# A two-layer graph network on one core: node products made ahead of the neighbour lists, the last lists made inside layer 0

## The chip, the cores and the metric

The kernel runs on one NeuronCore of a Trainium2 chip. The core has a matrix engine (PE, whose weight loads are shown apart as PEld), a vector engine (DVE), a scalar engine (ACT), GpSimd (POOL) and a sync engine (SP) that here only issues transfers. Sixteen DMA engines move data between HBM and the on-chip memory SBUF. [...] The metric is the device time of one execution in microseconds, the median of several.

## The reference: what is computed

Inputs are 4096 nodes with 512 features (x), a 4096 x 4096 matrix adj of 0 and 1 in int32 (64 MB, about four ones in a row), and weights.

```python
# layer 0: attention with 8 heads of 64
Wh = einsum('nf,hfo->hno', x, W)
f1 = einsum('hno,ho->hn', Wh, a[:, :64]); f2 = einsum('hno,ho->hn', Wh, a[:, 64:])
e  = where(adj > 0, leaky_relu(f1[:, :, None] + f2[:, None, :], 0.2), -9e15)
x  = layernorm(x + softmax(e) @ Wh)
# layer 1: mean of the neighbours, two linear maps and a third over both
agg = (adj > 0) @ x / max(deg, 1)
out = concat([x @ W_self + b_self, agg @ W_nb + b_nb]) @ W_comb + b_comb
x   = layernorm(x + relu(out))
```

## The kernel before: tiling, stages and order

The kernel does not multiply by adj. It turns each row of adj into a short list of neighbours and then gathers rows. Nodes are worked in 32 blocks of 128. The instruction order on every engine is the order of the program text (`manual_schedule`), each engine works its own instructions in that order, and waits between engines follow from the data and from the reuse of buffers.

1. *Start.* w_sb holds W with 16 more columns, the products of W with the two halves of a, so that one matmul gives f2, Wh and f1 together. DVE makes these columns (L722, L727). PE multiplies W_nb by the lower half of W_comb into m2 (`fold_weights`, L251 and L262) and the bias (`fold_bias`, L279): layer 1 then needs one product with m2 and one with m1 instead of four.
2. *Lists* (loop at L746, one step a block). SP loads adj in halves of 1 MB (`load_adj`, four buffers, so two blocks) and x eight blocks ahead. ACT turns a half into 0 and 1 in bf16 (`mask_adj`, L367), waiting for its transfer. PE turns x (`transposed`, L304; ACT copies the result), makes the node row in two halves (`node_half`, L312) and between them packs the mask into keys (`fold_adj`, L379). DVE copies the halves into a row (L316) and finds the largest keys (`max_keys`, L393). The row goes to the table t0 in HBM by a transfer that ACT issues; rows have two buffers, so a row waits for the transfer of the one before the last. Every fourth step starts a `decode` of four blocks: a generator of DVE work, of which one part is done in each of the next steps (L402 to L487) with two small PE products (L436, L463). Its results are the indices to gather (idx), the extra places of rows with over three neighbours (es) and the degrees. A node with more than three neighbours borrows one of 256 extra places of its block.
3. *The turn.* When the last row of t0 is in HBM, POOL starts the gathers of t0 (`gather`, L508: five indirect transfers a block). DVE finishes the decodes of the last eight blocks, and PE makes m1 from W_self and the upper half of W_comb, one piece at a time.
4. *Layer 0* (loop at L800, step i works on blocks i-1 to i+3 at different stages). DVE forms attention weights (`a_weights`: L532 for the first three neighbours, L536 for the extra places) and weighs the gathered rows (L580 to L611); PE adds the extra places (L595) and sums of weights (L546); ACT does exp and the normalization (L618 to L627); PE turns the new x block and multiplies it by m2 (`a_z`, L632), and the result goes to the table t1 in HBM.
5. *Layer 1* (loop at L876). Gathers of t1, the product with m1 (`g_self`, L656), the extra places (L663), mean, relu and normalization.

A flag tells at the end whether the short form was allowed (at most 256 extra places, values in bounds); otherwise a dense form runs, which these inputs do not reach.

Of the kernel before, what the change touches and what calls it, by code (L numbers as in the profile page):

```python
# [39 lines left out]
P = 128  # L40
# [7 lines left out]
K0 = 3  # L48
# [36 lines left out]
def listed_layers(  # L85
# [32 lines left out]
    EX = KX + 2 + 1 + H  # L118
# [89 lines left out]
    es = const.tile([P, NB, KH, EX], F32, name="es")  # L208
    idx = const.tile([P, NB, KS], U32, name="idx")
# [4 lines left out]
    m1 = const.tile([P, FB, HD], F32, name="m1")  # L214
    brow = const.tile([P, HD], F32, name="brow")
    bc = const.tile([1, HD], F32, name="bc")
# [13 lines left out]
    def load_fold(k, w, fp):  # L230
        wr = fp.tile([P, FB, HD], F32, name="wr")
        (nc.sync, nc.scalar)[k].dma_start(wr, w.rearrange("(c p) o -> p c o", p=P))
        wc = fp.tile([P, FB, HD], F32, name="wc")
        (nc.sync, nc.scalar)[k].dma_start(
            wc, w_comb[k * HD : (k + 1) * HD, :].rearrange("(c p) o -> p c o", p=P)
        )
        return wr, wc
# [6 lines left out]
    def fold_weights(loaded, m, wp, tag="pw", last=None):  # L244

        wr, wc = loaded

        def turned(c):
            tp = ps.tile([P, FB, P], F32, name="nm", bufs=2)
            for d in range(FB):  # L250
                nc.tensor.transpose(tp[:, d, :], wr[:, c, ts(d, P)], ident)  # L251
            t = wp.tile([P, FB, P], F32, name="xT", bufs=2)
            nc.scalar.copy(t, tp)
            return t

        wT = turned(0)
        for c in range(FB):
            nxt = turned(c + 1) if c + 1 < FB else last and last()
            t = "pw" if c + 1 < FB else tag
            mp = ps.tile([P, HD], F32, name=t, bufs=2 if t == "pw" else 1)  # L260
            for d in range(FB):
                nc.tensor.matmul(  # L262
                    mp, lhsT=wT[:, d, :], rhs=wc[:, d, :], start=(d == 0), stop=(d == FB - 1)
                )
                if t != "pw" and d == FB // 2 - 1:
                    yield
            nc.scalar.copy(m[:, c, :], mp)
            wT = nxt
            yield

    def fold_bias(loaded, brw, to, tag):
# [5 lines left out]
        bp = ps.tile([1, HD], F32, name=tag, bufs=1)  # L277
        for d in range(FB):
# [4 lines left out]
            if d == FB // 2 - 1:  # L283
                yield
        nc.vector.tensor_add(brow[0:1, :], bp, to)
# [9 lines left out]
    def load_x(b, xacc):  # L295
        if b < NB:
            nc.sync.dma_start(xs[:, b, :], x[ts(b, P), :])
            nc.gpsimd.tensor_tensor(xacc, xacc, xs[:, b, :], OP.add)  # L298
# [19 lines left out]
    def node_rest(b, row):  # L318
# [3 lines left out]
        )  # L322

    def mean_row(w_sb, xacc, wp):
# [7 lines left out]
        nc.vector.tensor_copy(xm, pm)  # L332
        mr = wp.tile([P, HD], F32, name="y", bufs=2)
        mf = small.tile([1, H], F32, name="mf", bufs=1)
        for k in range(2):
# [9 lines left out]
            if k == 0:  # L345
                nc.vector.tensor_copy(mf, pq[:, 0:H])
        nc.scalar.dma_start(t0[1:2, 0:H], mf)
        nc.scalar.dma_start(t0[1:2, H:TW], mr[0:1, :])

# [3 lines left out]
    def load_adj(b, ap):  # L353

        if b < NB:
            for h in range(NH):
                at = loads[b, h] = ap.tile([P, NG // NH, SC], I32, name="at", bufs=4)
                r = b * P + h * (P // NH)
                nc.sync.dma_start(
                    at, adj[r : r + P // NH, :].rearrange("(j r) (s c) -> (r s) j c", r=RG, s=SEG)  # L360
                )

    def mask_adj(b, h, ap):
        if b == NB:
            return
# [29 lines left out]
    def decode(b0, dp, wp):  # L395
# [48 lines left out]
        if b0 + G == NB:  # L444
            yield
        for b in range(b0, b0 + G):
            lt = wp.tile([P, KH * P], F32, name="st", bufs=2)
            nc.vector.tensor_scalar(lt, iota[:, 0 : KH * P], end[:, b : b + 1], None, OP.is_lt)
            if b0 + G < NB:
                st = wp.tile([P, KH * P], F32, name="own", bufs=4)  # L450
            else:
                if b % 2 == 0:
                    rows = wp.tile([P, FW], F32, name="row", bufs=2)
                st = rows[:, b % 2 * KH * P : (b % 2 + 1) * KH * P]
# [5 lines left out]
        pe = ps.tile([P, G, KH, EX], F32, name="sm", bufs=2)  # L460
# [6 lines left out]
        if b0 + G == NB:  # L467
            yield
        nc.vector.tensor_copy(es[:, bs], pe)
# [35 lines left out]
    def gather(table, b, gp):  # L505
        g = gp.tile([P, KS, TW], F32, name="g")
# [22 lines left out]
    def a_weights(b, wp):  # L529
        gw = G0[b][:, :, 0:H]  # L530
        e = E[b] = wp.tile([P, KS, H], F32, name="e", bufs=3)
        nc.vector.tensor_tensor(  # L532
            e[:, 0:K0, :], gw[:, 0:K0, :],
            lst[:, b, KL + 3 :].unsqueeze(1).to_broadcast([P, K0, H]), OP.add,
        )
        nc.vector.tensor_add(e[:, K0:KS, :], gw[:, K0:KS, :], es[:, b, :, KX + 3 :])  # L536
# [149 lines left out]
    wp = ctx.enter_context(tc.tile_pool(name="work", bufs=1))  # L686
    dp = ctx.enter_context(tc.tile_pool(name="decode", bufs=1, side="right"))
    ap_cm = tc.tile_pool(name="lists", bufs=1, side="right")
    ap = ap_cm.__enter__()
    xa = ctx.enter_context(tc.tile_pool(name="xa", bufs=1))  # L690
    xacc = xa.tile([P, FIN], F32, name="xacc")
    nc.gpsimd.memset(xacc, 0.0)
    w_sb = xa.tile([P, FB, FW], F32, name="w_sb")
    with tc.tile_pool(name="wa", bufs=1) as wa:
        arow = wa.tile([1, H, 2, D], F32, name="arow")
        nc.scalar.dma_start(arow, a0.rearrange("h (k d) -> h k d", k=2).unsqueeze(0))
        for h in range(H):
            nc.sync.dma_start(
                w_sb[:, :, H + h * D : H + (h + 1) * D], w0[h].rearrange("(c p) o -> p c o", p=P)
            )  # L700
        loaded = load_fold(1, w_nb, wa)
        brw = load_bias(1)
        nc.scalar.dma_start(bc, b_comb.rearrange("(a o) -> a o", a=1))
        load_x(0, xacc)
        load_x(1, xacc)
        load_adj(0, ap)
        load_x(2, xacc)
        load_x(3, xacc)
        load_adj(1, ap)
        for b in range(4, XL):  # L710
            load_x(b, xacc)
        pads(wp)
        av = []
        for k in range(2):
            av.append(ps.tile([P, H, D], F32, name=("key", "sm")[k], bufs=(1, 2)[k]))
            nc.tensor.matmul(av[k], lhsT=oner, rhs=arow[:, :, 1 - k, :], start=True, stop=True)
        for a in range(2):
            for k in range(2):
                for c in range(FB):
                    pr = wa.tile([P, H // 2, D], F32, name="pr", bufs=2)  # L720
                    cs = slice(H + a * HH, H + (a + 1) * HH)
                    nc.vector.tensor_mul(  # L722
                        pr, w_sb[:, c, cs].rearrange("p (h d) -> p h d", d=D),
                        av[k][:, a * 4 : a * 4 + 4, :],
                    )
                    f = k * TW + a * 4
                    nc.vector.tensor_reduce(w_sb[:, c, f : f + 4], pr, AX.X, OP.add)  # L727
        last = {}

        def first():  # L730
            last["xT"] = transposed(0, wp)

        pieces = fold_weights(loaded, m2, wp, last=first)
        for c in range(FB):
            next(pieces)
            if 1 <= c <= 2:
                mask_adj(0, c - 1, ap)
        next(pieces, None)
        for _ in fold_bias(loaded, brw, bc, "key"):
            pass  # L740
    fp = ctx.enter_context(tc.tile_pool(name="fold", bufs=1))


    xT = last["xT"]
    row, lists = None, []
    for b in range(NB):  # L746
        load_x(b + XL, xacc)
        load_adj(b + 2, ap)
        if b == NB - 2:
            loaded = load_fold(0, w_self, fp)  # L750
            brw = load_bias(0)
        if b < NB - 1:
            for p in lists:
                next(p, None)
        mask_adj(b + 1, 0, ap)
        nxt = transposed(b + 1, wp) if b + 1 < NB else None
        if b > 0:
            nc.scalar.dma_start(t0[2 + (b - 1) * P : 2 + b * P, :], row[:, 0:TW])
        mask_adj(b + 1, 1, ap)
        row = wp.tile([P, FW], F32, name="row", bufs=2)  # L760
        node_half(b, 0, xT, w_sb, row)
        fold_adj(b, dp)
        max_keys(b)
        node_half(b, 1, xT, w_sb, row)
        node_rest(b, row)
        xT = nxt
        if b == NB - 1:
            for p in lists:
                next(p, None)
        if b % G == G - 1:  # L770
            lists = [*lists[-1:], decode(b + 1 - G, dp, wp)]
        if b == NB - 4:
            mean_row(w_sb, xacc, wp)
    nc.scalar.dma_start(t0[2 + (NB - 1) * P : 2 + NB * P, :], row[:, 0:TW])
    ap_cm.__exit__(None, None, None)
    gp = ctx.enter_context(tc.tile_pool(name="gat", bufs=GA, side="right"))
    for b in range(3):
        G0[b] = gather(t0, b, gp)
# [513 lines left out]
```

## Time and profile before

| | |
|---|---|
| median of 3 runs | 727.04 us (726.87 to 727.1) |
| profiled span | 725.5 us |
| busy PE / DVE / ACT / POOL | 650.8 / 493.5 / 430.3 / 348.5 us |
| moved by DMA | 191.29 MB, mean 264 GB/s |
| start, until the first node product (L312) | 38.4 us |
| lists, until the last node row | to 242.5 us |
| turn, until the first product with m2 (L632) | to 287.5 us |
| layer 0, until the last product with m2 | to 506 us |
| layer 1 | to 725 us |

The stages have different limits, so the busy shares of the whole span say little. Read each stage for itself: which engine is full in it, and what the others wait for. An engine's idle time counts only where the chain of work runs through that engine.

### The profile page before, as it was taken

What the parts mean: (1) busy time and instruction counts of PE and PEld (TensorE: products, weight loads), DVE (VectorE), ACT (ScalarE), POOL (GpSimd) and SP (SyncE); (2) the same over time, 40 slices, a digit from 0 to 9 for tenths busy, and PEclk for the clock granted to TensorE, in tenths of its full rate; (3) what the DMA queues carried; (4) which work ended last, traced back from release to release, by engine and by line L of the source; (5) the groups of instructions that cost most, each with busy time, mean ns of one, the idle gap of its engine ahead of it and who ended that gap; (6) DMA issues with size and microseconds to landing.
All of it is one profiled execution on the core that took longest, in us unless ns stands there. A gap on an engine that the chain in (4) does not pass through costs nothing.

```text
span 725.5 us, 9190 instructions
## 1 busy us (share of the span) xinstructions
PE 650.8 (90%) x2654; PEld 358.1 (49%) x2654; DVE 493.5 (68%) x1474; ACT 430.3 (59%) x883; POOL 348.5 (48%) x368
## 2 busy tenths in 40 slices
PE   4998888887899899999999999998999999999972
PEld 1465656655666654555555555554444444443320
DVE  5236777877877676899999999994255555554552
ACT  1566667666677123565766657665466666666653
POOL 3421122122100377566666666500677777777771
PEclk9999999999999889999999999999999999999995
DMA  9979999999999477677787887711588888878882
GB/s 278 358 279 394 393 393 392 392 393 392 392 393 389 163 211 211 185 230 230 226 234 225 230 230 229 227 41 39 173 257 250 252 252 255 251 249 249 250 256 101
DMA packets 84248, 191.29 MB, mean 264 GB/s; under 512 B 12496, under 2 KB 12504, under 8 KB 84190
## 3 DMA queue, kind: packets, MB, share of 16 engines
q0 software_dynamic: 25600, 84.56, 40.6%
q1 hardware_dynamic: 52896, 95.43, 35.7%
q10 hardware_dynamic: 5694, 10.64, 4.0%
q8 instruction: 23, 0.38, 0.2%
q14 instruction: 35, 0.29, 0.1%
HBM read 165.29 MB, written 25.31 MB: 263 GB/s over the span
## 4 chain that ended last, share of the span: by engine, by line
PE 50%; DMA 19%; POOL 10%; issue 9%; DVE 6%; ACT 5%; ACTq 0%; POOLq 0%; SPq 0%; DVEq 0%
PE pw L632 16%; POOL g L508 10%; DMA at<-in_adj_dram 9%; PE nm L595 8%; PE pw L312 7%; DMA g<-t,idx 6%; ACT xT L306 3%; PE pw L262 3%; PE tp L304 3%; DMA t<-row 2%; PE pw L663 2%; PE sm L546 2%; PE sm L463 1%; DMA w_sb<-in_L_gnn_W_dram 1%; PE nm L656 1%
## 5 line engine op out<-in xcount | busy, mean ns | idle before, releaser
L508 POOL DMA_INDIRECT g<-t,idx x320 | 303.3, 948 | 211.8 <-issue 120.2
L367 ACT ACTIVATE ab<-at 128x2048 bf16<-128x2048 int32 x64 | 122.2, 1910 | 62.9 <-DMA at<-in_adj_dram 56.1
L312 PE MATMUL pw<-w_sb,xT 128*128 128x264 f32 x512 | 127.6, 393 | 0.0
L632 PE MATMUL pw<-m,xT 128*128 128x512 f32 x256 | 118.4, 605 | 3.4 <-ACT xT L306 1.7
L298 POOL TENSOR_TENSOR xacc<-xacc,xs 128x512 f32<-128x512 f32 x32 | 41.3, 1292 | 148.7 <-DMA xs<-in_x_dram 148.2
L312 PEld LDWEIGHTS pw<-w_sb,xT 128*128 128x128 f32 x512 | 92.2, 190 | 26.1 <-issue 3.8
L306 ACT COPY xT<-tp 128x512 f32<-128x512 f32 x80 | 46.2, 578 | 72.1 <-PE tp L304 71.9
L580 DVE TENSOR_TENSOR g<-g,key 128x1024 f32<-128x1024 f32 x64 | 77.8, 1216 | 1.1
L632 PEld LDWEIGHTS pw<-m,xT 128*128 128x128 f32 x256 | 46.0, 189 | 56.8 <-issue 45.9
L304 PE MATMUL tp<-ident,xs 128*128 128x128 f32 x320 | 49.5, 277 | 26.3 <-ACT xT L306 25.3
L304 PEld LDWEIGHTS tp<-ident,xs 128*128 128x128 f32 x320 | 37.9, 141 | 61.0 <-ACT xT L306 32.2
L595 PE MATMUL nm<-g,own 128*128 128x512 f32 x128 | 62.7, 612 | 0.0
L656 PE MATMUL nm<-m,xT 128*128 128x512 f32 x128 | 57.7, 593 | 1.3 <-ACT xT L306 1.3
L656 PE MATMUL pw<-m,xT 128*128 128x512 f32 x128 | 57.6, 592 | 0.0
L316 DVE COPY row<-pw 128x264 f32<-128x264 f32 x64 | 27.3, 427 | 41.7 <-DMA t<-row 17.5
L642 ACT COPY sm<-g 128x512 f32<-128x512 f32 x32 | 18.9, 590 | 50.8 <-DMA g<-t,idx 47.8
L648 DVE TENSOR_TENSOR y<-sm,g 128x512 f32<-128x512 f32 x32 | 22.1, 691 | 30.8 <-DMA g<-t,idx 30.5
L663 PE MATMUL pw<-g,own 128*128 128x512 f32 x64 | 34.2, 651 | 9.0 <-DMA g<-t,idx 6.0
L663 PE MATMUL nm<-g,own 128*128 128x512 f32 x64 | 34.1, 641 | 8.4 <-DMA g<-t,idx 4.1
L656 PEld LDWEIGHTS nm<-m,xT 128*128 128x128 f32 x128 | 23.1, 190 | 24.5 <-issue 23.0
L646 DVE TENSOR_TENSOR sm<-sm,g 128x512 f32<-128x512 f32 x32 | 22.3, 697 | 18.6 <-DMA g<-t,idx 17.8
L670 DVE SCALAR_TENSOR_TENSOR sm<-y,lst,nm 128x512 f32<-128x512 f32 x16 | 12.1, 755 | 33.5 <-PE nm L663 33.5
(176 smaller groups left out, 1006.0 us busy)
## 6 DMA issues: line engine op xcount, KB each, us to landing
at<-in_adj_dram SPq DMA_DIRECT2D x64, 1024.0 KB, 10.8
t<-row ACTq DMA_DIRECT2D x32, 260.0 KB, 5.7
xs<-in_x_dram SPq DMA_DIRECT2D x32, 256.0 KB, 6.0
t<-row SPq DMA_DIRECT2D x32, 256.0 KB, 3.4
out_dram<-row SPq DMA_DIRECT2D x32, 256.0 KB, 3.7
g<-t,idx POOLq DMA_INDIRECT x320, 4.1
w_sb<-in_L_gnn_W_dram SPq DMA_DIRECT2D x8, 128.0 KB, 7.6
wr<-in_L_gnn_W_nb_dram ACTq DMA_DIRECT2D x1, 1024.0 KB, 7.2
```

Source lines behind the costliest of these rows:

```text
L298: nc.gpsimd.tensor_tensor(xacc, xacc, xs[:, b, :], OP.add)
L304: nc.tensor.transpose(tp[:, c, :], xs[:, b, ts(c, P)], ident)
L306: nc.scalar.copy(t, tp)
L312: nc.tensor.matmul(pw, lhsT=xT[:, c, :], rhs=w_sb[:, c, k * HW : (k + 1) * HW], start=(c == 0), stop=(c == FB - 1),)
L316: nc.vector.tensor_copy(row[:, k * HW : (k + 1) * HW], pw)
L367: nc.scalar.activation(ab, loads.pop((b, h)), AF.Relu, accum_out=asum[:, b, h : h + 1])
L508: nc.gpsimd.indirect_dma_start(out=g[:, k, 0 : table.shape[1]], out_offset=None, in_=table[:, :], in_offset=bass.IndirectOffsetOnAxis(ap=i ...
L580: nc.vector.tensor_tensor(gv if to is None else to.rearrange("p (k h d) -> p k h d", k=1, h=H), gv, E[b][:, sl].unsqueeze(3).to_broadcast( ...
L595: nc.tensor.matmul(NM[b], lhsT=OWN[b][:, k, :], rhs=G0[b][:, K0 + k, H:TW], start=False, stop=(k == KH - 1), skip_group_check=b > 1,)
L632: nc.tensor.matmul(pz, lhsT=xT[:, c, :], rhs=m2[:, c, :], start=(c == 0), stop=(c == FB - 1))
L656: nc.tensor.matmul(NM[b], lhsT=xT[:, c, :], rhs=m1[:, c, :], start=False, stop=False, skip_group_check=True,)
L663: nc.tensor.matmul(NM[b], lhsT=OWN[b][:, k, :], rhs=g[:, K0 + k, 0:HD], start=False, stop=(k == KH - 1), skip_group_check=True,)
```

## The change

Four things are moved.

- *Wh ahead of the lists.* The list loop now has 28 steps and makes 32 node blocks: in steps 3, 10, 17 and 24 (`AHEAD`) it makes two. t0 is so complete when the lists of 28 blocks are made. The adj of the last four blocks is loaded and masked after the loop: two are loaded at its end, one in the turn, one in step -1 of layer 0. Their decode is done one part a step from step 2 of layer 0 on.
- *Weight products.* m2 and its bias are no longer made at the start: the weights are loaded in step 12 of the lists, half of m2 and the bias is made in steps 14 to 20, the rest in the turn. m1 and its bias move from the turn to the end of layer 0 and behind it.
- *First loads.* Half of W is loaded from the ACT queue, and the load of the fold weights no longer stands ahead of x and adj. The columns of w_sb are made with four products and four sums of four times the size; GpSimd does half of the products. The mean row, needed for nodes without neighbours, is made in parts earlier in the loop.
- *Smaller edits.* f1 of each block and of its extra places is kept in one tile (f1s), so that `a_weights` needs one add instead of two. adj buffers lie in two pools, gathered rows in two, so that memory can pass from one use to the next.

The diff, cut to its core:

```diff
-    EX = KX + 2 + 1 + H
+    EX = KX + 2 + 1
+    AHEAD = (3, 10, 17, 24)
+    LB = NB - len(AHEAD)
...
-    def fold_weights(loaded, m, wp, tag="pw", last=None):
+    def fold_weights(loaded, m, wp, tags):
         wr, wc = loaded
...
+        for c in range(FB):
+            tp = ps.tile([P, FB, P], F32, name="sm", bufs=2)
             for d in range(FB):
                 nc.tensor.transpose(tp[:, d, :], wr[:, c, ts(d, P)], ident)
+            wT = wp.tile([P, FB, P], F32, name="wT", bufs=1)
+            nc.scalar.copy(wT, tp)
+            yield
...
             nc.scalar.copy(m[:, c, :], mp)
-            wT = nxt
             yield
...
+        nc.gpsimd.tensor_copy(
+            f1s[:, b, 0:K0, :], lst[:, b, KL + 3 :].unsqueeze(1).to_broadcast([P, K0, H])
+        )
...
-        nc.vector.tensor_copy(es[:, bs], pe)
+        nc.vector.tensor_copy(es[:, bs], pe[:, :, :, 0:EX])
+        nc.vector.tensor_copy(f1s[:, bs, K0:KS, :], pe[:, :, :, EX:])
...
-        nc.vector.tensor_tensor(
-            e[:, 0:K0, :], gw[:, 0:K0, :],
-            lst[:, b, KL + 3 :].unsqueeze(1).to_broadcast([P, K0, H]), OP.add,
-        )
-        nc.vector.tensor_add(e[:, K0:KS, :], gw[:, K0:KS, :], es[:, b, :, KX + 3 :])
+        nc.vector.tensor_add(e, gw, f1s[:, b])
...
+    for h in range(H):
+        (nc.sync, nc.scalar)[h // (H // 2)].dma_start(
+            w_sb[:, :, H + h * D : H + (h + 1) * D], w0[h].rearrange("(c p) o -> p c o", p=P)
+        )
...
+    for a in range(2):
+        times(nc.gpsimd, a, 1, av[:, 1])
+        times(nc.vector, a, 0, pa[0])
+        summed(a, 0)
+        summed(a, 1)
...
-    for b in range(NB):
-        load_x(b + XL, xacc)
-        load_adj(b + 2, ap)
+    for b in range(LB):
+        for k in range(1 + (b in AHEAD)):
+            load_x(w + k + XL)
+            sum_x(w + k + XL, xacc)
+        load_adj(b + 2, aps)
+        if b == 12:
+            loaded = load_fold(1, w_nb, fp)
+            todo = [fold_bias(loaded, brw)]
+        if b == 16:
+            m2s = fold_weights(loaded, m2, fp, ("sm", "sm", "pw", "pw"))
+        if b == 21:
+            todo = [mean_row(w_sb, xacc, wp)]
+        some(lists)
...
+        row = node_block(w, xT, b)
+        w, xT = w + 1, nxt
+        if b in AHEAD:
+            nxt = transposed(w + 1, wp)
+            store(w - 1, row)
+            row = node_block(w, xT)
+            w, xT = w + 1, nxt
+        elif b >= 14:
+            some(todo)
+            if 16 <= b < 21:
+                some([m2s])
...
+    load_adj(LB + 2, aps)
+    mask_adj(LB + 1, 0, ap)
+    mask_adj(LB + 1, 1, ap)
...
     for b in range(3):
-        G0[b] = gather(t0, b, gp)
-    folds = fold_weights(loaded, m1, wp, "tp")
+        G0[b] = gather(t0, b, gps)
+    fold_adj(LB, dp)
+    max_keys(LB)
     some(lists)
-    some([folds])
+    some([m2s])
+    fold_adj(LB + 1, dp)
+    some(lists)
+    max_keys(LB + 1)
+    some([m2s])
+    some(lists)
+    some(lists)
+    some([m2s])
+    some(lists)
+    some(lists)
     a_owners(0, wp)
     a_owned(0, wp)
...
+    some([m2s])
+    late = decode(LB, dp, lambda: sp)
...
-        if i == -1 or i == 0:
-            some([folds])
...
+        if i == -1 or i == 0:
+            for h in range(NH):
+                mask_adj(LB + 3 + i, h, ap)
+            if i == -1:
+                load_adj(NB - 1, aps)
+        if i == 0 or i == 1:
+            fold_adj(LB + 2 + i, dp)
+            max_keys(LB + 2 + i)
         if i == 1:
-            spread_bias()
...
+            loaded = load_fold(0, w_self, fp)
+            brw = load_bias(0)
+            m1s = fold_weights(loaded, m1, fp, ("key", "key", "tp", "key"))
+            bias = fold_bias(loaded, brw)
+        if i > 1:
+            some([late])
+        if i == NB - 4 or i == NB - 3:
+            some([bias])
+        if i == NB - 2:
+            some([m1s])
+        if i == NB - 1:
+            some([m1s])
+            some([m1s])
+    for _ in m1s:
+        pass
+    spread_bias()
```

## The prediction

> **What bounds the kernel now.** I read the slices of the span first, then the chain that ended last, then the busy time by stage, then the order of single instructions where stages meet.
>
> ```profile
> PE   4998888887899899999999999998999999999972
> DVE  5236777877877676899999999994255555554552
> DMA  9979999999999477677787887711588888878882
> GB/s 278 358 279 394 393 393 392 392 393 392 392 393 389 163 211 211 185 230 230 226 234 225 230 230 229 227 41 39 173 257 250 252 252 255 251 249 249 250 256 101
> ```
>
> A slice is 18.1 us. Slices 4 to 13 hold the lists: the transfer rate stands at 392 to 394 GB/s whatever PE does. From slice 16 to 26 (layer 0) PE and DVE both show 9 and the rate is 230. After slice 28 (layer 1) no engine is full, and the chain below names the gathers.
>
> ```profile
> PE 50%; DMA 19%; POOL 10%; issue 9%; DVE 6%; ACT 5%; ACTq 0%; POOLq 0%; SPq 0%; DVEq 0%
> PE pw L632 16%; POOL g L508 10%; DMA at<-in_adj_dram 9%; PE nm L595 8%; PE pw L312 7%; DMA g<-t,idx 6%; ACT xT L306 3%; PE pw L262 3%; PE tp L304 3%; DMA t<-row 2%; PE pw L663 2%; PE sm L546 2%; PE sm L463 1%; DMA w_sb<-in_L_gnn_W_dram 1%; PE nm L656 1%
> ```
>
> Busy time by stage (columns: stretch, length, then busy us and instructions of PE, weight loads, DVE, ACT, POOL; granted clock, DMA share, GB/s):
>
> ```profile
> 110.67:137.50 26.83, 22.37 (x149) 16.08 (x148) 20.53 (x80) 17.90 (x21) 5.18 (x4) 1.00 1.05 393
> 216.00:240.00 24.00, 23.64 (x153) 16.32 (x155) 15.51 (x70) 17.08 (x20) 0.00 (x0) 1.00 1.02 380
> 240.00:287.00 47.00, 41.95 (x157) 23.77 (x146) 34.04 (x118) 8.70 (x23) 31.11 (x33) 0.85 0.63 182
> 302.00:497.00 195.00, 193.03 (x721) 104.54 (x721) 180.28 (x467) 125.87 (x335) 113.23 (x120) 1.00 0.70 203
> 497.00:531.00 34.00, 31.34 (x92) 14.91 (x92) 10.94 (x32) 17.29 (x40) 16.05 (x17) 1.00 0.46 140
> ```
>
> The first line is four list blocks: 6.7 us each, the DMA full, PE with 4.5 us to spare. The second is the end of the lists, where x is all loaded: PE is full. The third is the turn. The fourth is 28 blocks of layer 0 at 6.97 us: PE idles 1%, DVE 8%. The pace is PE's; its one bubble, and DVE's own wait for PE, are here:
>
> ```profile
> 489.94 0.69 DVE L611 SCALAR_TENSOR_TENSOR y<-y,nm 128x512 f32<-128x512 f32 x1 [0.38 <-PE nm L595]
> 491.02 3.70 PE L632 MATMUL pw<-m,xT 128*128 128x512 f32 x8 [0.33 <-ACT xT L306]
> ```
>
> The marks that I compare below: the last row of Wh leaves DVE at 242.46, the first attention weights start at 263.01, the first layer-0 product with m2 at 287.50, the last at 502.41, the first layer-1 gather at 509.78.
>
> ```profile
> 242.46 0.43 DVE L316 COPY row<-pw 128x264 f32<-128x264 f32 x1 [1.07 <-PE sm L436]
> 263.01 0.18 DVE L532 TENSOR_TENSOR e<-g,lst 128x24 f32<-128x24 f32 x1
> 287.50 3.70 PE L632 MATMUL pw<-m,xT 128*128 128x512 f32 x8
> 502.41 3.70 PE L632 MATMUL pw<-m,xT 128*128 128x512 f32 x8 [0.73 <-ACT xT L306]
> 509.78 0.94 POOL L508 DMA_INDIRECT g<-t,idx  x1 [41.56 <-issue]
> ```
>
> **What the Trainium skill says.** "TensorE: Matmul & The Clock Gate", Part 1, says that PE falls to half rate after an idle window of about 3.4 us and needs as long to recover; the trace agrees: granted clock 0.50 in 248 to 252, behind a PE that was busy 2.4 of 4 us from 240, and L262's first group takes 4.85 us there against 3.44. "DMA: Bandwidth & Descriptors", "Issuing engines are not separate DMA queues", says a second issuing engine saves only issue time; before, the eight w_sb issues hold the sync queue for 8.35 us, so about 4 can be saved and no bandwidth won. "Perfetto Trace Analysis", "Optimizing Scalar/DVE Operations", says that grouping small operations saves the fixed overhead, and that work moved from VectorE to GPSIMD may not help as they share a read port. In the trace the two small adds of L532 and L536 start 0.09 us apart, so merging them is worth 0.1 us of DVE per block.
>
> **Part 1, start and list phase.** Before, m2 (L262) and the bias hold PE until 38.0; the 16 product pairs hold DVE from 11.09 to 23.7. After, PE waits only for the columns of w_sb: two GpSimd products of 1024 elements (2 x 2.5, twice the 1.29 of L298) alternating with DVE sums (1.2 each, by L580's 1.22 for 1024), 7.4 us behind w_sb at about 9.5: 17 us instead of 38.
>
> That is not 21 us of gain, since the DMA sets the first half. Adjacency block 14 lands at about 123 before. After, until it lands: 15 blocks x 2.097 = 31.5 MB, 23 x blocks 6.0, w_sb 1.05, 14 stores 3.7, together 42.2 MB, at 393 GB/s 107 us, plus 5.5 lost at the start (before moves 3.5 MB in its first 14 us, 393 GB/s would be 5.5 MB; its further 6 to 7 us, lost when PE lagged, go away): 113. Block 15 comes behind the 2.1 MB of w_nb and w_comb, moved to here: 4.7 MB, 12 us, 125. With the mask (2.1) its fold starts at 127.
>
> From there PE is the bound. Prices from the row of single instructions: a list step with its node block 4.96, a node block alone 4.2, decode matmuls 2.1 per four blocks, a quarter of m2 3.95, mean row 4.7, bias 3.6. Left: 12 steps 59.5, two extra blocks 8.4, rest of step 15 2.5, bias 3.6, two quarters of m2 7.9, mean row 4.7, decode 6.3: 93 us, and 2 for stalls (rows waiting for stores cost DVE 17.5 us in nine waits before, mostly hidden): 222 against 242.4. **Gain 20.4.** The bounds: 212 if the DMA sets the end (78.3 MB, 199 + 5.5, and a last step of 7), 229 if waits of row stores and heavy steps add.
>
> **Part 2, the turn.** DVE has the same decode to do as before (20.6 us from the last row to L532), with two max_keys of 0.9 more and small waits less: 21.4. New is that the last quarter of m2 stands on PE between a_owned(0), which DVE frees only at the end of the decode, and the first shared sum (L546): 3.4 us at full clock, 5 at half; I take 3.5. **Loss 4.3.** The two extra folds (0.76 each) and the quarter ahead of them lie in PE's wait for DVE; the gathers (5 x 1.25 a block from about 225) are ahead.
>
> From the first shared sum to the first m2 product: 23.7 us before (263.8 to 287.5), with 8.4 of m1 and bias matmuls, 3.1 of list matmuls and half clock in PE's queue. After, DVE sets it: 1.0, two steps of 6.4 and 7.3 with max_keys, 1.0 of handovers: 15.7. Then ACT: the masks of blocks 30 and 31 (4.2 each) stand ahead of xT(0), and block 31 can be loaded only when 30's masks free the buffers. Landing takes 5.6 (shortest) to 10.8 us (median under full load); I take 7, so ACT is held 2 us (bounds 0 and 6). 17.7, **gain 6.0**; spread_bias leaves the second step, 1.2 more.
>
> **Part 3, late lists in layer 0.** The decode of the last four blocks costs DVE 2.8, 3.4, 1.4, 4.2 (in two parts), 1.9: 13.8 us, read from 249.6 to 263 of before, one part a step. DVE's slack is 0.5 a step and 0.1 from the merged add. Seven steps x 0.6 = 4.2, and about 1 us of phase before PE notices. 13.8 + 0.9 (max_keys) - 5.2: 9.5. PE's 2.1 us of list matmuls lie in the same delay. **Loss 9.5** (5 to 15). Later steps don't win it back, as PE sets their pace.
>
> **Part 4, m1 at the end.** The bias (3.6 + 0.2) falls on step 29, still full; a transpose 0.5, then a product and a transpose (3.9) stand ahead of the last m2 product. **Loss 8.2.** The other five parts, 3 x 3.44 + 2 x 0.5 and 2.4 of waits for the single wT buffer, 13.8, come behind it and hide: the gathers of layer 1 start 3.6 us after the last m2 product, run 25 x 1.25 us before they need a buffer back, at 34.9; PE gives it back at 13.5 (its delay before) + 13.8 + 1.5 = 28.8. PE takes 5.6 a block (167.4 in 30) against 6.25 of gathers, so the lag is gone by the end. Cost 0. The row of f1 copies on POOL and the split copy of es lie in slack of the lists: 0.
>
> **Sum.** 727.0 - 20.4 + 4.3 - 6.0 - 1.2 + 9.5 + 8.2 = **721.4**.
>
> **Rivals.** *Well hidden* (13%): the lists end at the DMA's 212 and half the late decode fits phase slack: 721.4 - 10 - 5 = 706. For it: two blocks of buffers; against: PE's heavy steps of 9 us. *A draw* (12%): ACT is held 6 us and stalls of the lists cost 2 more: 727. *Slower* (25%): the work moved to layer 0 is paid in full (decode 15, masks +4) and the lists end at 229: 721.4 + 5.5 + 4 + 7 = 738, or half of that, 731. For it: layer 0 has 0.33 us of PE slack a step while the lists had 1.1. *Mine* has 50%. Faster in all 0.63, same 0.11, slower 0.26. For 8 in 10 I reach from 711 to 732.
>
> **What would show it.** First node matmul near 17; rate 390 until about 125, then below, PE at 9; last row at 222; first weights at 243 to 244, a PE product of m2 before the first shared sum; ACT waiting for block 31's transfer; steps 2 to 8 of layer 0 longer than 6.97 by 9 together; the last m2 product 8 us later than the pace. I am wrong if the lists stay on the DMA's pace to the end, if layer 0 keeps 6.97 through the late decode, or if POOL waits for PE early in layer 1.

## The result, and the profile after

The changed kernel takes 738.55 us (median of 4 runs, 738.22 to 742.05), the kernel before 727.07 beside it. The ratio of the single runs is 1.0167 (of the medians 1.0158), interval 1.0135 to 1.0198: it is slower by 1.7%, clear of the noise, where 721.4 was forecast. Runs over 1.5% above the fastest of the same kernel are left out of the medians and ratios of this document. The profiled run spans 736.5 us (before: 725.5).

The slices of the span after (PE, DVE, DMA, GB/s):

```profile
PE   3788896999997749889999999999899999999872
DVE  3538767468679575999999999973036656655552
DMA  7999999999988796666777887500578888888882
GB/s 241 391 393 393 392 393 391 393 394 344 363 291 306 211 328 220 203 188 199 217 231 229 233 227 230 171 28 29 155 212 259 255 253 263 260 255 249 255 253 92
```

A slice is 18.4 us. The full transfer rate ends at slice 9 (counted from 0) instead of 13, and PE stands at 9 from there to slice 11: the second half of the lists is now PE's, as forecast. DVE has its row of nines in layer 0 as before, but in slices 16 and 17 PE, the bound there before, shows an 8. The chain that ended last covers 1% of this run, so it is not used; I compare marks and stages instead. Stages (columns as in the prediction: stretch, length, then busy us and instructions of PE, weight loads, DVE, ACT, POOL; granted clock, DMA share, GB/s):

```profile
110.67:137.50 26.83, 19.80 (x107) 12.74 (x106) 15.85 (x67) 14.83 (x17) 5.60 (x7) 0.87 1.05 391
180.00:207.00 27.00, 27.00 (x173) 18.46 (x172) 18.18 (x76) 18.28 (x22) 0.61 (x3) 1.00 0.93 329
240.00:287.00 47.00, 32.63 (x121) 17.11 (x121) 26.77 (x79) 18.97 (x40) 30.81 (x33) 0.78 0.75 235
302.00:360.00 58.00, 53.23 (x203) 28.98 (x202) 53.49 (x153) 31.82 (x84) 33.48 (x36) 0.96 0.67 189
360.00:480.00 120.00, 119.04 (x447) 64.76 (x447) 110.95 (x279) 78.04 (x208) 75.00 (x80) 1.00 0.75 218
```

First the DMA is full and PE has 7 us to spare; then PE is full (27.00 of 27) at 329 GB/s. In the turn PE works 32.6 of 47 us. The last two lines are layer 0 with and without the late decode: PE idles 8% in the first, 1% in the second.

The marks of the prediction, in the same order (node row, attention weights, m2's last quarter, the wait that it ends in, first and last product with m2, first gather of layer 1):

```profile
225.76 0.41 DVE L311 COPY row<-pw 128x264 f32<-128x264 f32 x1
244.60 0.20 DVE L526 TENSOR_TENSOR e<-g,f1s 128x40 f32<-128x40 f32 x1
244.99 5.15 PE L258 MATMUL pw<-wc,wT 128*128 128x512 f32 x8
250.93 0.18 DVE L545 TENSOR_REDUCE dn<-e 128x8 f32<-128x24 f32 x1 [5.90 <-ACT e L530]
275.89 5.14 PE L622 MATMUL pw<-m,xT 128*128 128x512 f32 x8 [8.50 <-ACT xT L301]
512.31 3.70 PE L622 MATMUL pw<-m,xT 128*128 128x512 f32 x8 [0.78 <-ACT xT L301]
519.97 0.94 POOL L502 DMA_INDIRECT g<-t,idx  x1 [50.23 <-PE sm L251]
```

Line 5 is the finding: PE waited 8.50 us for the turned x block that ACT had to copy. What ACT did meanwhile is its mask of block 31, twice held by the transfer, and then the copy:

```profile
266.27 1.91 ACT L366 ACTIVATE ab<-at 128x2048 bf16<-128x2048 int32 x1 [2.61 <-DMA at<-in_adj_dram]
273.37 1.91 ACT L366 ACTIVATE ab<-at 128x2048 bf16<-128x2048 int32 x1 [5.09 <-DMA at<-in_adj_dram]
275.27 0.56 ACT L301 COPY xT<-tp 128x512 f32<-128x512 f32 x1
```

The transfer had been issued at 256.73 and 258.62, as its buffers came free. The DMA was nearly full from then on (share 0.97), with 3.4 MB of gathers beside the 2.1 MB of block 31 (columns as above):

```profile
256.73:273.40 16.67, 9.79 (x42) 4.88 (x40) 14.56 (x38) 6.73 (x14) 12.40 (x15) 0.81 0.97 331
```

| mark | before | forecast | after | missed since the mark above |
|---|---|---|---|---|
| first node product | 38.38 | 17 | 22.56 | not on the path |
| last node row | 242.46 | 222.1 | 225.76 | +3.7 |
| first weights | 263.01 | 243.5 | 244.60 | -2.6 |
| first shared sum | 263.82 | 247.7 | 250.95 | +2.1 |
| first m2 product | 287.50 | 265.4 | 275.89 | +7.2 |
| second m2 product | 295.67 | 272.4 | 285.21 | +2.3 |
| last m2 product | 502.41 | 496.8 | 512.31 | +2.7 |
| end of span | 725.5 | 719.9 | 736.5 | +1.1 |

The forecast column is the prediction's sum, carried from mark to mark; its end is the device time less the 1.5 us by which the span is shorter. At the first m2 product the change is still 11.6 us ahead; a layer later it is 9.9 behind. A mark of one run is good to about 1 us only: in after and the four kernels that differ from it by one edit, whose lists are the same, the last row comes between 224.61 and 226.91.

### The profile page after: what moved, and what is told of

Same layout as the page of the kernel before. It is cut to its first block, busy times and chain, and to the rows that moved or that the text cites. A ratio compares the mean times of both kernels' runs of the same rounds, so it can differ in the third digit from the quotient of the medians.

```text
span 736.5 us, 9226 instructions
## 1 busy us (share of the span) xinstructions
PE 653.0 (89%) x2654; PEld 364.4 (49%) x2654; DVE 484.2 (66%) x1424; ACT 429.2 (58%) x884; POOL 359.8 (49%) x402
## 5 line engine op out<-in xcount | busy, mean ns | idle before, releaser
L307 PE MATMUL pw<-w_sb,xT 128*128 128x264 f32 x512 | 129.9, 400 | 4.5 <-POOL wc L722 4.5
L622 PE MATMUL pw<-m,xT 128*128 128x512 f32 x256 | 121.2, 618 | 11.5 <-ACT xT L301 10.3
L307 PEld LDWEIGHTS pw<-w_sb,xT 128*128 128x128 f32 x512 | 94.6, 194 | 30.4 <-POOL wc L722 4.9
L622 PEld LDWEIGHTS pw<-m,xT 128*128 128x128 f32 x256 | 47.6, 196 | 65.4 <-issue 47.8
L570 DVE TENSOR_TENSOR g<-g,key 128x1024 f32<-128x1024 f32 x64 | 77.9, 1217 | 1.1
L299 PE MATMUL tp<-ident,xs 128*128 128x128 f32 x320 | 51.1, 284 | 23.8 <-ACT xT L301 23.8
L299 PEld LDWEIGHTS tp<-ident,xs 128*128 128x128 f32 x320 | 39.6, 146 | 54.1 <-ACT xT L301 27.5
L646 PE MATMUL pw<-m,xT 128*128 128x512 f32 x128 | 57.6, 593 | 0.0
L318 POOL COPY f1s<-lst 128x24 f32<-128x24 f32 x32 | 6.7, 208 | 66.8 <-DVE fmax L315 34.8
L660 DVE SCALAR_TENSOR_TENSOR sm<-y,lst,pw 128x512 f32<-128x512 f32 x16 | 12.1, 755 | 39.7 <-PE pw L653 39.7
L653 PE MATMUL pw<-g,own 128*128 128x512 f32 x64 | 32.1, 626 | 5.9 <-DMA g<-t,idx 5.9
```

The costliest lines, as they stand in the source:

```text
L299: nc.tensor.transpose(tp[:, c, :], xs[:, b, ts(c, P)], ident)
L307: nc.tensor.matmul(pw, lhsT=xT[:, c, :], rhs=w_sb[:, c, k * HW : (k + 1) * HW], start=(c == 0), stop=(c == FB - 1),)
L570: nc.vector.tensor_tensor(gv if to is None else to.rearrange("p (k h d) -> p k h d", k=1, h=H), gv, E[b][:, sl].unsqueeze(3).to_broadcast( ...
L622: nc.tensor.matmul(pz, lhsT=xT[:, c, :], rhs=m2[:, c, :], start=(c == 0), stop=(c == FB - 1))
L646: nc.tensor.matmul(NM[b], lhsT=xT[:, c, :], rhs=m1[:, c, :], start=False, stop=False, skip_group_check=True,)
L653: nc.tensor.matmul(NM[b], lhsT=OWN[b][:, k, :], rhs=g[:, K0 + k, 0:HD], start=False, stop=(k == KH - 1), skip_group_check=True,)
```

## The experiments

Theory A: each piece is paid at the stage that receives it, as a separate term: the hold of ACT by block 31's transfer about 8 us, the late decode 12, m1 8.4, m2's last quarter some 3. The rivals stand in each expectation. The kernel before took 727.1 to 727.5 us beside the runs of this section, so times can be compared with 738.55.

**Mask of block 31 one step later** (all of its work moves with it):

```diff
-        if i == -1 or i == 0:
+        if i == -1 or i == 1:
             for h in range(NH):
-                mask_adj(LB + 3 + i, h, ap)
+                mask_adj(LB + 2 + (i > 0), h, ap)
...
-        if i > 1:
+        if i > 2:
             some([late])
```

> After, with the two masks of block 31 (and its fold and max_keys, and the start of the late decode) one step later in the text, so that ACT does not stand before block 31's transfer. Theory A (ACT in program order holds PE for this transfer, 2.6 + 5.1 us): the first m2 product comes at about 268 instead of 275.9, ACT's wait for adj at 273 is gone, and the time is 730 to 732 against 738.5. Rival B (the DMA is full with gathers and the last adj block in this window, and DVE and PE wait for gathers anyway): the wait only changes its name to one for g, time 736 to 739.

730.52 us, ratio to before 1.0048 (1.0028 to 1.0067): 8.0 less (6.5 between the two profiled runs). The trace, with the next m2 product as third line:

```profile
269.24 0.59 ACT L301 COPY xT<-tp 128x512 f32<-128x512 f32 x1 [4.84 <-PE tp L299]
269.87 0.30 PEld L622 LDWEIGHTS pw<-m,xT 128*128 128x128 f32 x2 [0.29 <-ACT xT L301]
278.52 3.70 PE L622 MATMUL pw<-m,xT 128*128 128x512 f32 x8 [1.56 <-ACT xT L301]
```

ACT now waits for PE, not for the DMA, and PE's wait for xT is 0.29. From the first shared sum to the first m2 product it is 17.25 us instead of 24.94: 7.7 less, the hold of 2.61 + 5.09. The transfer was no faster here (its second half landed 14.9 us after issue); the masks came at 274.09 with nothing to wait for. They are not free there: they stand ahead of the next xT copy, and PE waits 1.56 for it. Theory A holds; B falls.

**Late decode in finer parts** (more `yield`s, one part of about 0.8 us a step):

```diff
             nc.vector.max(nb[:, g, 8:16], kj[:, g, :])
+            if fine and g < G - 1:
+                yield
...
-    late = decode(LB, dp, lambda: sp)
+    late = decode(LB, dp, lambda: sp, True)
```

> After, with the late decode cut into 19 parts of about 0.8 us, one a step from step 2 to step 20 of layer 0, in place of 7 parts of up to 3.4 us. Theory A (DVE has 0.5 us of slack a step and everything over it is paid): 19 x 0.3 = 6 us paid instead of 12, time 732 to 734. Rival C (the late decode costs by its PE products and waits, not by the size of its DVE parts): steps stay 12 us longer in sum, time 737 to 740.

736.13 us, 1.0124 (1.0101 to 1.0147): 2.4 less, about half of what A expected. The excess over 6.976 us a step is 8.7 us (from the third m2 product to the nineteenth) against 12.0 in after. In the profiled run the layer also began 3.0 later (second m2 product at 288.24 against 285.21), about half of that because the granted clock stood at half for longer and the first m2 product took 6.59 us (5.14 in after); so the last m2 product is only 0.1 earlier, and the 1.8 us by which this span is shorter lie in layer 1, for which I have no cause. So the gain is read from the steps, not from the end.

What slack has DVE? The trace of after shows it where the decode has ended, DVE is late, and L601 waits for nothing:

```profile
352.60 0.68 DVE L601 SCALAR_TENSOR_TENSOR y<-y,nm 128x512 f32<-128x512 f32 x1
359.39 0.68 DVE L601 SCALAR_TENSOR_TENSOR y<-y,nm 128x512 f32<-128x512 f32 x1
```

At its own pace DVE needs 6.79 us a step; PE's pace is 6.976, so the slack is 0.19. The steps of the late decode, less their part of it, also take 6.78 to 6.80 in nearly every case, in both kernels; one step of each waits 0.4 us longer for PE. The parts, from the first instruction of one to the next instruction behind it, take 12.8 us in after and 11.8 here (18 parts, one less than I had counted): 12.8 + 0.4 - 7 x 0.19 = 11.9 (measured 12.0), 11.8 + 0.4 - 18 x 0.19 = 8.8 (measured 8.7). A's mechanism holds with well under half the slack I gave it; C falls, as the same products of PE cost 3.3 us less when DVE's parts are smaller.

**m1 and its bias all behind layer 0:**

```diff
-        if i == NB - 4 or i == NB - 3:
-            some([bias])
-        if i == NB - 2:
-            some([m1s])
-        if i == NB - 1:
-            some([m1s])
-            some([m1s])
+    for _ in bias:
+        pass
     for _ in m1s:
```

> After, with m1's bias and all eight pieces of m1 behind the last m2 product, none in steps 28 to 31 of layer 0. Theory A (PE is the bound of layer 0, and behind it PE has a lead of gathers to wait for): the last m2 product comes 8.4 us earlier, about 504; PE returns the first gather buffer of layer 1 about 2 us after POOL wants it, so 1 to 3 us are lost there: time 731 to 733. Rival D (what moves behind layer 0 is paid in layer 1 in full, since PE is late for the whole of it): time 737 to 739.

736.36 us, 1.0118 (1.0099 to 1.0138): 2.2 less. The last m2 product came at 503.55, 8.8 earlier, but layer 1 took 224.3 us from its first gather instead of 216.5, with this wait of POOL for a buffer that PE returns late:

```profile
550.13 0.94 POOL L502 DMA_INDIRECT g<-t,idx  x1 [7.95 <-PE key L299]
```

Nearer to D than to A, outside both ranges: the gathers' lead holds the five pieces that after puts there, and no more.

**Last quarter of m2 earlier in the turn:**

```diff
     some([m2s])
     some(lists)
+    some([m2s])
     some(lists)
     a_owners(0, wp)
     a_owned(0, wp)
-    some([m2s])
```

> After, with the last quarter of m2 ahead of the last part of the decode of blocks 24 to 27 in the turn, so that it lies in PE's wait for DVE and ACT's copy of m2 does not stand ahead of the first exp. Theory A: first shared sum at about 246 instead of 251, first m2 product and end 4 to 5 us earlier, 734. Rival E (the turn is set by block 31's transfer, as the wait at 273 ends last whatever comes before): the earlier shared sum only lengthens ACT's wait for adj, time 737 to 739; but as the load is issued behind the masks of block 30, which come earlier too, a part of the gain may pass.

736.16 us, 1.0128 (1.0109 to 1.0147): 2.4 less. The first shared sum came at 248.72 (2.2 earlier, of which 1.15 is an earlier last row), the first m2 product at 271.88. The edit did only part of what it was for: the quarter ran mostly at half clock (granted clock 0.57 over its 6.4 us), ACT's copy of it (247.67) still stood ahead of the first exp, DVE still waited 4.85 for it, and ACT was still held by the transfer:

```profile
241.20 6.44 PE L258 MATMUL pw<-wc,wT 128*128 128x512 f32 x8
248.70 0.18 DVE L545 TENSOR_REDUCE dn<-e 128x8 f32<-128x24 f32 x1 [4.85 <-ACT e L530]
269.35 1.91 ACT L366 ACTIVATE ab<-at 128x2048 bf16<-128x2048 int32 x1 [6.05 <-DMA at<-in_adj_dram]
```

Of the 4.0 us at that mark 1.9 are left at the last m2 product: steps 0 and 3 of layer 0 became longer (10.7 and 12.2 us against 9.3 and 9.4). Both fell under the half clock: the granted clock is 0.50 from 267.24 to 277.48 and the first m2 product takes 6.46 us (5.14 in after), and again from 304.79 to 311.62, in after from 299.30 to 306.13. The verdict lies between A and E; what the quarter costs in the turn is shown below, by a kernel that has none of m2 there.

**All four edits:**

> After with the four single edits together, on another chip than its first try. Theory A (separate terms that add): 738.5 - 8.0 - 2.4 - 2.2 - 2.4 = 723.5. Rival (they share one wait): 727 to 730.

723.61 us, 0.9950 (0.9937 to 0.9963). The four single gains are 8.0 + 2.4 + 2.2 + 2.4 = 15.0; together they make 14.9. Each gain is known to 1.4 to 1.7 us only, but 727 to 730 is ruled out: the costs behave as separate terms.

**The four edits, and Wh ahead sooner** (`AHEAD = (2, 5, 8, 11)`):

> The four edits, and the extra Wh blocks in steps 2, 5, 8 and 11 of the lists. On the disturbed chip its last row came 5.5 us earlier than that of the four edits alone, as Theory A had it (4 to 6). Theory A here: the same, and 4 to 6 us in the time, 718 to 720. Rival: the turn takes it back, within 1 us of the four edits.

720.52 us, 0.9902 (0.9887 to 0.9916): 3.1 less, short of A's 4 to 6. Its last node row comes 5.0 us earlier (220.75), the first m2 product 2.6. PE work moved from the half of the lists where PE is full to the half where the DMA is shortens the lists; half of it is lost in the turn.

**The ahead part undone** (`AHEAD = ()`: 32 list steps, all decodes end in the turn; all else as in after):

> After with one part undone: no Wh block is made ahead, all 32 blocks are listed in 32 steps and their decodes end in the turn as before (the mean row is made from step 24 on, when x is complete); weight products, first loads and smaller edits stay. The first try of this ran on a chip on which the kernel before takes 795.7 us, with waits of 6 to 11 us in the turn and layer 1 that no kernel shows elsewhere; there the last row came at 237.5. Theory A: last row at 237, turn 45 us or less, no excess in layer 0 but the 8.4 at its end: a_z(0) at 278 to 282, time 722 to 727. Rival F (the ahead part is what gains): 735 to 745.

725.65 us, 0.9964 (0.9947 to 0.9980), as A had it:

```profile
236.91 0.42 DVE L311 COPY row<-pw 128x264 f32<-128x264 f32 x1
```

Making Wh ahead ends the lists 11.1 us sooner (225.76). At the first m2 product 2.4 of it are left, and after the late decode the kernel is 11.9 behind (eleventh m2 product at 359.99 against 348.1). All told the ahead part costs 738.55 - 725.65 = 12.9 us; the other parts are worth 1.8 (725.65 against 727.46, the kernel before in the same session).

**m2 made in the lists' slack as well** (no Wh ahead):

```diff
-        if b == 12:
+        if b == 2:
             loaded = load_fold(1, w_nb, fp)
...
+        if b in (5, 6, 9, 10, 13, 14, 17, 18):
+            some([m2s])
```

> No Wh made ahead, and all of m2 made in the first 18 steps of the lists (its weights loaded in step 2, one transpose and one product in every fourth step, bias in steps 20 and 21), none in the turn. Theory A (PE has 4.5 us to spare in four list steps while the DMA is full, so m2's 16 us cost nothing there, and the DMA's bytes are the same): the last row comes at 226 to 230, as early as with Wh made ahead, the first shared sum 21 to 22 us later, a_z(0) at 264 to 270, layer 0 without excess but 8.4 at its end: time 709 to 716, below both. Rival G (the lists are PE's from start to end once m2 is in them, or the DMA loses what PE delays): last row at 235 to 240 and 722 to 727.

719.30 us, 0.9891 (0.9875 to 0.9907). Two windows of it, late in the lists and in the turn:

```profile
180.00:207.00 27.00, 26.19 (x169) 18.16 (x168) 21.43 (x87) 19.41 (x24) 3.36 (x6) 1.00 1.05 390
236.00:256.00 20.00, 6.93 (x36) 6.25 (x35) 15.00 (x65) 0.51 (x2) 12.89 (x14) 0.57 0.58 161
```

My time was 3 us off and the last row wrong: 236.05, not 226 to 230. I had left out the bytes: 67.1 MB of adj, 8.4 of x, 8.5 of rows, 1.0 of w_sb, 2.1 of weights are 87.1 MB, at 393 GB/s 222 us, plus 5.5 at the start and a last step of 7: 234.5. The first window shows both PE and DMA full. Still, three more pieces of m2 (two products of 3.6 us and a transpose) in the lists did not move their end (236.91 without), and the first shared sum came 6.4 us earlier. From the first weights to the first shared sum it is 1.23 us here, 7.59 without this edit and 6.35 in after: the last quarter of m2 costs 5 to 6 us at that place, where Theory A had some 3.

**And the bias and first quarter of m1 in the turn**, three quarters behind layer 0:

```diff
     for k in range(7):
         some(lists)
+        if k < 2:
+            some([m1s])
+        if k in (1, 2):
+            some([bias])
```

> The same kernel as in the run before (bias and first quarter of m1 in the turn, three quarters behind), on another chip; that run fell on one where the kernel before takes 799.5. Theory A: step gaps of layer 0 all 6.98, turn 0 to 3 longer, time 710 to 715. Rival H (m1 is paid wherever it is put): 718 to 722.

712.33 us, 0.9808 (0.9786 to 0.9829), below both kernels. It ran on another chip than the run before, where the kernel before takes nearly the same time (727.11 against 727.46), and the intervals of the two ratios do not meet. The same turn, and the first gather of layer 1:

```profile
236.00:256.00 20.00, 14.10 (x49) 7.13 (x48) 14.71 (x63) 1.24 (x3) 13.04 (x14) 0.82 0.59 166
494.59 0.94 POOL L503 DMA_INDIRECT g<-t,idx  x1 [41.68 <-issue]
```

PE's 7.2 us more in the turn cost 2.1 (first shared sum at 257.21 against 255.06); the last m2 product comes 6.6 earlier (487.10), and layer 1 takes 214.6 us, so nothing is given back. What m1 costs is a matter of the place. H falls.

Where the kernels stand at the marks (last row, first shared sum, first and last m2 product, first gather of layer 1):

| kernel | us | row | shared | first m2 | last m2 | gather |
|---|---|---|---|---|---|---|
| before | 727.07 | 242.46 | 263.82 | 287.50 | 502.41 | 509.78 |
| after | 738.55 | 225.76 | 250.95 | 275.89 | 512.31 | 519.97 |
| mask later | 730.52 | 226.91 | 252.62 | 269.87 | 506.2 | 513.84 |
| four edits | 723.61 | 225.76 | 248.79 | 265.3 | 490.5 | 498.12 |
| and Wh sooner | 720.52 | 220.75 | 243.79 | 262.73 | 487.9 | 495.53 |
| no Wh ahead | 725.65 | 236.91 | 261.47 | 278.30 | 500.4 | 508.03 |
| and m2 in lists | 719.30 | 236.05 | 255.06 | 271.71 | 493.7 | 501.07 |
| and m1 in turn | 712.33 | 235.61 | 257.21 | 273.5 | 487.10 | 494.59 |

**Runs on two other chips.** Four first tries fell on a chip on which the kernel before takes 795.7 us, the fifth on another, on which it takes 799.5. Their expectations:

> After with one part undone: no Wh block is made ahead, all 32 blocks are listed in a loop of 32 steps and their decodes end in the turn as before; weight products, first loads and the smaller edits stay as in after. Theory A (the ahead part shortens the lists by only a few us, as PE has the same node work in either order, and pays 8 us for the hold of ACT and 12 for the late decode): last node row at 229 to 232 instead of 225.8, no excess in layer 0 but the 8.4 at its end, time 720 to 725. Rival F (the ahead part is what shortens the lists: without it the last row is back at 240, and the late decode only moves into the turn): 735 to 745.

> The kernel without Wh made ahead, and the last quarter of m2 ahead of the last two parts of the decode in the turn, so that ACT's copy of it does not stand ahead of the first exp. Theory A: the 2.2 to 4 us that the first shared sum wins reach the first m2 product in full here, since no transfer of adj is left in the turn to take them: 3 to 4 us below the kernel without this edit. Rival E: the turn is set by something else (the gathers, DVE), 0 to 1 us.

> After with the four single edits together (masks of block 31 one step later, late decode in 19 parts, m1 behind layer 0, last quarter of m2 earlier). Theory A (the costs are separate terms and add): 738.5 - 8.0 - 2.4 - 2.2 - 2.4 = 723.5, perhaps 2 less, as the earlier quarter of m2 is no longer followed by a wait for the transfer. Rival (they share one wait, so that the second of two edits gains nothing): 727 to 730.

> The kernel of the four edits together, and the four extra Wh blocks made in steps 2, 5, 8 and 11 of the lists instead of 3, 10, 17 and 24. Theory A (the DMA is the bound of the first half of the lists, PE that of the second, so two blocks of PE work, 8.4 us, pass into PE's slack of the first half, and the x rows and rows of t0 that are moved there as well cost 2.7 us of DMA): last node row 4 to 6 us earlier, time 4 to 6 us below the four edits alone. Rival (the lists are already on PE's pace in both halves, or the transfers lose what PE wins): within 1 us of it.

> The kernel without Wh ahead and with all of m2 in the lists' slack (719.3), and the bias and the first quarter of m1 made in the turn, where PE is busy 6.9 of 20 us, the other three quarters behind the last m2 product; nothing of m1 is left in layer 0's steps. Its first weights are loaded behind the last adj block and loaded once more in layer 0. Theory A (8.4 us of PE are paid at the end of layer 0 because PE is full there, and only there): step gaps of layer 0 all 6.98, the last m2 product 8 us earlier, 6 pieces behind it hide in the gathers' lead as 5 did, the turn loses 0 to 3: time 710 to 715. Rival H (m1 is paid wherever it is put, in the turn because PE at half clock holds the decode's small products, or behind because POOL then waits for PE as it did 8 us with all of m1 behind): 718 to 722.

Measured against before there: without Wh ahead 787.58 (0.9906, 0.9879 to 0.9933), the same with m2 earlier 795.60 (0.9981, 0.9964 to 0.9998), four edits 802.48 (1.0076, 1.0051 to 1.0101), with Wh sooner 798.30 (1.0011, 0.9986 to 1.0037), m1 in the turn 794.63 (0.9920, 0.9888 to 0.9951). In the first two the mean row is made in step 21 from the x of 30 blocks, so the last two are left out of it. The absolute times of the expectations say nothing there. Against the ratios of the repeats, three of the four repeated kernels stand 1.1 to 1.3 points worse, the one without Wh ahead 0.6 better. These runs hold waits of 6 to 11 us in the turn and in layer 1 that no other run shows, so their order is not used. The second of them was not repeated: what m2 earlier is worth without Wh ahead stays open.

## Why the prediction was wrong

*Bound of the stages: right.* PE's last long wait of the lists (6.67 us, for an xT copy that stood behind the mask of block 15) ended at 128.9, and block 15's fold started at 132.8 (forecast 127); PE is at 9 from there, last row 3.7 late. The order of the two bounds was well seen, a term of 20.4 measured 16.7, and from the last row to the first weights DVE took 18.8 us instead of the 21.4 of the forecast, which gave 2.6 back. The first node product at 22.56 instead of 17 is not seen in the time, as the transfer rate was at 391 GB/s from slice 1 on; ACT's copy of the a-row product stood 13.5 us until the transfer of the bias row had landed.

*The failed step is in Part 2, "Landing takes 5.6 (shortest) to 10.8 us (median under full load); I take 7, so ACT is held 2 us (bounds 0 and 6)".* The two loads were issued at 256.73 and 258.62, and the masks could start at 266.27 and 273.37: the halves of block 31 landed about 9.5 and 15 us after issue, because both halves shared the DMA with the gathers, which moved more bytes than they did (3.4 against 2.1 MB). ACT was held 2.61 + 5.09 = 7.7 us instead of 2, beyond the upper bound of 6, with the xT copy and so all of PE's next step in its queue. The forecast gain of 6.0 became a loss of 1.2, missed by 7.2; the hold is 5.7 of that. The other 1.5 is there without the hold too (17.25 us in the kernel with the mask later, where the forecast without a hold was 15.7); in this stretch PE ran at half clock (0.50 from 254.93 to 261.75), but no run separates that. Taking only the hold away brought 8.0 us in the time. It does not turn the sign: that kernel still takes 3.3 us more than before, and the misses below make up the rest. The Trainium skill's "Trainium Architecture — The Big Picture", "Inside one NeuronCore", says that each engine has its own instruction stream and meets the others only through semaphores. The trace agrees, and shows a price: a mask that nothing needed yet, waiting for its transfer, held every later instruction of ACT. I saw that queue, and priced the wait by transfers that had the DMA in another mix.

*m2's last quarter, same part: right in kind, too small.* It took 5.15 us, at half clock, where I took 3.5 of the bounds 3.4 and 5; and ACT's copy of it stood ahead of the first exp, so DVE waited 5.90 us. Missed 2.1; as the kernel without m2 in the turn shows, the whole price of this place is 5 us and more.

*"spread_bias leaves the second step, 1.2 more": wrong.* It left, but the step became 9.3 us (8.2 before), 2.3 more than the forecast. PE ran at half clock after its wait, 5.14 us for the m2 product instead of 3.70, and the fold of block 31 had come into the step (0.8 us). So 1.4 of the 2.3 belongs to the hold as well. In the kernel with the mask later the step is still 8.6 us, but for another reason: neither the half clock nor the fold is in it, and PE waits 1.56 for the xT copy behind the masks.

*Part 3, late decode: right mechanism, size 12.0 instead of 8.6 (9.5 less the 0.9 of max_keys, which fell into the step before).* The term that failed is "Seven steps x 0.6 = 4.2, and about 1 us of phase": I took the mean idle of 0.52 and the merged add for slack. DVE had 0.19 a step, 1.3 in all, and no phase. The parts took 12.8 us instead of 13.8, and DVE waited 0.4 for PE in one of them. In the two steps from 352.60 on DVE was late, and yet busy only 12.70 of 13.60 us: about 0.45 us of idle a step stays, in gaps of at most 0.10 us. The merged add is worth 0.06 (1.49 us from L566 to the second L570; from L576 to the second L580 in before, 1.55). The parts stood ahead of L601 and left it no idle (the end of a part, then L601):

```profile
304.32 0.26 DVE L420 MAX8 nb<-kj 128x8 f32<-128x96 f32 x1
304.50 0.67 DVE L601 SCALAR_TENSOR_TENSOR y<-y,nm 128x512 f32<-128x512 f32 x1
```

*Part 4, m1: right.* Forecast 8.2 at the end of layer 0, measured 8.4 (from the eleventh m2 product to the last 152.3 us against 143.95). The five pieces behind it cost at most the 1.1 us that the end is late; once the gathers of layer 1 run, POOL waits no more than 0.3 us at a time. The bias is the first of these two, the last m2 product but two the second:

```profile
491.65 3.59 PE L273 MATMUL sm<-wc,bcol 128*1 128x512 f32 x8
496.51 3.70 PE L622 MATMUL pw<-m,xT 128*128 128x512 f32 x8 [0.33 <-ACT xT L301]
```

The sum of the misses, 3.7 - 2.6 + 2.1 + 7.2 + 2.3 + 2.7 + 1.1 = 16.5, is the whole difference of the spans but for rounding (736.5 - 719.9). The hold is 7.1 of it (5.7 and 1.4). The slower rival had the right total, 738, by other terms: it put the lists' end at 229 (225.76), and the masks at 4 us more where they cost 7.1 more. That is luck in the total.

Some readings of the prediction were loose and carried nothing: DVE's parts in Part 3 add up to 13.7, DVE shows 9 in slices 17 to 26 only (counted from 0), and L262's groups take 4.97 and 3.60 us in the timeline. "The trace agrees", of the clock, is too strong: PE's longest idle time ahead of the half clock was 2.11 us, and it took 6.8 us to recover (last section).

## What to carry to other kernels

"Perfetto Trace Analysis", "Optimization Strategy", of the Trainium skill says that interleaving stages with different limits may help. Here it did where the receiving stage had the engine free (m2 in the DMA-bound half of the lists, m1 in the turn: 13 us below the kernel without Wh ahead) and it cost nearly its full price where that engine was over 90% busy (12.8 us of DVE work, 12.0 paid: 92% was full).

Price a moved load by the traffic that it will meet, and look at what stands behind its consumer in that engine's queue; if something urgent does, place the consumer one step later.

Slack is the step of the bound less the step that the engine needs at its own pace (6.976 - 6.79), not the engine's mean idle time.

## What was not expected of the hardware

A transfer of 1 MB that shared the DMA with gathers landed about 15 us after its issue; the page "DMA: Bandwidth & Descriptors" of the Trainium skill, "Measured", has 6.15 us of DMA time for 1 MB, which says nothing of a transfer among others, and the measurement decides here.

The half clock came without a long pause, and stayed. In before (columns as above) the granted clock fell behind 3.41 us in which PE was busy a third of the time, and took 6.82 us to recover though PE was busy throughout:

```profile
242.02:245.43 3.41, 1.14 (x8) 0.73 (x6) 2.79 (x12) 0.00 (x0) 0.00 (x0) 1.00 0.21 78
245.43:252.25 6.82, 6.82 (x23) 5.12 (x24) 5.16 (x18) 1.17 (x2) 4.89 (x5) 0.50 0.48 127
```

How busy PE is does not tell when it falls: in the kernel with the mask later it fell behind a stretch with 2.74 us busy of 3.41 (226.42 to 229.83), and did not fall behind one with 1.43 (704.28 to 707.70). What decides is open.

Two chips took 8.5 to 12% longer with every kernel that ran on both kinds (795.7 and 799.5 us for before) at a granted clock of 0.93 to 0.95 against 0.96 to 0.98, too small a difference for it. In the kernel without Wh ahead, on the first of them, DVE waited 77.6 us in eight waits of layer 1 that the profile puts down to no engine of this core. What causes it is not known.
